# GAT and relational-attention layers: the fourth quad's scores, the masks and the affine steps in other places of a turn

## The chip, the cores and the metric

The kernel runs on one core of one Trainium2 chip. The metric is the device time of one execution in microseconds. The figures below are the times of the kernel before and one execution of it that the hardware profiler took.

## What is computed

The reference runs 64 graphs of 256 nodes with 256 features through two layers in float32. Cut to what matters here:

```python
# layer 0
h = gat(gat(x, adj))                  # two graph attentions, softmax over axis 1
h = layernorm(x + h) * g1 + b1
x = layernorm(h + relu(h @ wf1 + bf1) @ wf2 + bf2) * g2 + b2      # 256 -> 1024 -> 256
# layer 1
q, k = x @ Wq + bq, x @ Wk + bk                                   # 8 heads of 32
attn = softmax(q k^T / sqrt(32))
out = sum over r of (attn * (adj == r)) @ (x @ Wv[r] + bv[r])
x = layernorm(x + out @ Wo + bo) * g1 + beta1
x = layernorm(x + gelu(x @ W1 + b1) @ W2 + b2) * g2 + beta2
```

As `adj` is 0 or 1 here, two relations are enough: the kernel forms `e @ v0 + (e * adj) @ (v1 - v0)` and divides by the sum of `e` afterwards.

## The kernel before

**Turns.** Two graphs make a unit; there are 32 units (NG). `turn(y, x, z)` works on three units at once: the attention and the second layer of unit y, the first feed-forward of unit x = y + 1, the two graph attentions of unit z = y + 2. Turn 0 is the first; turns 1 to 29 have all three units and `middle` true; turn 30 has no z, turn 31 neither z nor x. In the code Y, X and Z are the units' tiles, and `if Z:`, `if X:`, `if middle:` choose between the variants.

**The order.** With `tc.manual_schedule` the instructions of PE (matmul), SP (DMA queue), DVE (vector) and ACT (scalar) go out in the order in which the code traces them; in turn 31 only those of PE and SP. Everything else, POOL (GpSimd) always, and DVE and ACT in turn 31, a planner places by its own costs, and it may slip such an instruction between ordered ones of an earlier turn. `with behind(...)` ties a block to a marked instruction. Buffers of a tag rotate: a new tile takes one that was released and waits for its last reader. The tag "g" has six PSUM banks, "po" and "zo" one each; e, ea and es have two buffers each.

**Attention of unit y.** `Projections` p forms q, k and v with seven products instead of eight; names such as "q5" or "v7" are these steps. Steps 1 and 2 (and 5 and 3; and 1, 6, 7, 4 in the other bank) share a bank: each step accumulates into it after the partial result of the step before has been taken, by an ACT copy (first time for a quarter of the output) or a DVE addition (second time), line 1040 or 1043. The same holds for the steps of the first feed-forward, `hidden_seven`, named "2a", "1a", ... "4b" (number of the product, half of the rows): "h1a" banks hold 1, 6, 7, 4 and "h1b" banks 2, 5, 3; the matmuls are line 900, the additions line 909, the copies line 912. Its moving operands tt are four differences (line 882). "ra" and "rb", "sa" and "sb" apply the activation on ACT.

The attention itself is cut in four **quads** (graph b, half m of the heads), numbers 0 to 3:
- `scores(n)`: 16 matmuls sp on 32x128 tiles (line 1076) into four banks, one for each head, and four exponentials on ACT (line 1085, `powers`), which release the banks;
- `masks(n)`: two DVE products of 128x1024, e with the adjacency (line 1089), for two heads each; `totals(n)`: one DVE addition (line 1094);
- `sums(n)`: 32 matmuls po (line 1104) and 8 matmuls zo (line 1107), on 128x32 tiles;
- `shares(b)`, after the two quads of graph b: `divided`, on DVE a transpose of zo, a reciprocal, a transpose back and a product with po (lines 1115 to 1120), with one addition on POOL (line 1117).

Then `out_(b)` multiplies by Wo. `project(z, ...)` (xpp, line 741) and others belong to unit z. `HiddenOut` out, with steps 1, 2, 5, 6, 3, 7, 4, is the second product of a feed-forward (yf, line 989): `product`, then `add` on DVE (line 997), `sums` for its operands (line 975).

**Norms and affine steps.** `norm` leaves mean and variance, POOL's power (lines 838, 839) the inverse deviation, `offsets` (DVE, line 846) mean times it, `applied_norm` normalizes on ACT (line 856). `affine` is `times` (line 865) and `plus` (line 868), both DVE on 128x1024. `waiting` holds unit y - 1 between its last product and its norm, its affine step and its store (`stored`, one DMA on SP); `late` holds affine steps that a turn leaves to the next: that of unit 0 for turn 0, and those of units 30 and 31 for turn 31. `piece()` is one step of unit 30's last product, done in turn 31.

**Around the change**, a middle turn has this order on PE: q and v steps with sp of quad 0 among them, sp of quad 1, sums 0, 2a 1a 5a, sp of quad 2, sums 1, 6a 3a 2b 1b 7a 5b 6b 4a 3b 7b, sp of quad 3, half of xpp, 4b, sums 2, sums 3, yop.

Of the kernel before, what the change touches and what calls it, by code (L numbers as in the profile page):

```python
# [385 lines left out]
def narrow_path(  # L386
# [22 lines left out]
    T = G * NB  # L409
# [438 lines left out]
    def applied_norm(y, blocks, mv, rs, nm, part=None, gpsimd=False):  # L848
        if part is None:
            offsets(blocks, mv, rs, nm)  # L850
        for t in part or blocks:
            if gpsimd:
                nc.gpsimd.tensor_scalar(y[:, t, :], y[:, t, :], rs[:, t:t + 1], nm[:, t:t + 1],
                                        op0=ALU.mult, op1=ALU.add)
                continue
            mark["normed"] = nc.scalar.activation(y[:, t, :], y[:, t, :], AF.Identity,  # L856
                                                  bias=nm[:, t:t + 1], scale=rs[:, t:t + 1])

    def affine(y, g_, b_):

        times(y, g_)
        plus(y, b_)
# [244 lines left out]
            nc.tensor.matmul(zo[a * DH:(a + 1) * DH, m * N:(m + 1) * N], ones, es[:, a, :],  # L1107
                             start=True, stop=True)

    def divided(u, b, po, zo, oT):  # L1110


        rz = work.tile([P, KB * N], F32, tag="es", name=f"rz{u}_{b}")
        rq = work.tile([P, KB * N // 32], F32, tag="rq", name=f"rq{u}_{b}")
        nc.vector.transpose(rz, zo)
        nc.vector.reciprocal(rq, rz.rearrange("p (n r) -> p n r", r=32)[:, :, 0])  # L1116
        nc.gpsimd.tensor_add(low, low, rq)  # L1117
        nc.vector.transpose(rz.rearrange("p (n r) -> p n r", r=32),
                            rq[:, :, None].to_broadcast([P, KB * N // 32, 32]))
        mark[f"divided{b}"] = nc.vector.tensor_tensor(  # L1120
            oT[:, :, b * N:(b + 1) * N], po.rearrange("p (m n) -> p m n", m=KB),
            rz.rearrange("p (m n) -> p m n", m=KB), ALU.mult)
# [95 lines left out]
    def turn(y_, x_, z):  # L1218
# [4 lines left out]
        q, k_, v = p.qk[:, :, 0], p.qk[:, :, 1], p.v  # L1223
        oT = q
        acc = [None] * G
        e, pe = {}, {}

        def scores(n, heads=range(HPB)):
# [9 lines left out]
        def totals(n):  # L1238
            e[n] = node_sums(*e[n])
# [4 lines left out]
                acc[b] = [psum.tile([P, 512], F32, tag=t_, name=f"{t_}{y_}_{b}") for t_ in ("po", "zo")]  # L1244
            applied(b, m, v, *e.pop(n), *acc[b])

        def shares(b):
            divided(y_, b, *acc[b], oT)

        def out_(b):  # L1250
            add_blocks(y_, "yop", y, b, lambda t, k: oT[:, k, t * P:(t + 1) * P],
# [2 lines left out]
        def first(names, ends=0):  # L1254

            if X:
                steps(names)
            else:
                for _ in range(ends):
                    piece()  # L1260
# [3 lines left out]
                                            ("PE", "SP", "DVE", "Activation")[:4 if X else 2]})  # L1264
        with order:
            p.sums()
            while late:
                affine(*late.pop(0))
            if X:
                n = X.pop("n")  # L1270
                offsets(*n)
# [35 lines left out]
            if X:  # L1307
                masks(0, (0,))
            if middle:
                p("q3 q7 v7")  # L1310
                masks(0, (2,))
            else:
                p("q6 v6 q7 v7")
                if X:
                    masks(0, (2,))
            if X:
                totals(0)
            else:
                with behind("projected"):
                    masks(0)  # L1320
                    totals(0)
            p("v3 q4 v4" if middle else "q4 v4")
            if waiting:
                last = norm(w, 3, wy, mv=last)
# [8 lines left out]
            if waiting:  # L1333
                first("2a 1a")
                applied_norm(wy, *last, [0, 1])
                first("5a")
                applied_norm(wy, *last, [2, 3])
            else:
                first("2a 1a 5a", 1)
            if Z:  # L1340
                early(z)
            scores(2)
            sums(1)
            first("6a")
            if X:
                shares(0)
            first("3a", 1)
            if not X:
                with behind("out"):
                    shares(0)  # L1350
            first("2b ra 1b")
            masks(2, (0,))
            first("7a")
            masks(2, (2,))
            first("5b sa 6b 4a")
            totals(2)
            first("3b rb 7b")
            if X:
                times(X["y"], rg1)
                plus(X["y"], rb1)  # L1360
            scores(3)
            first("sb", 2)
            masks(3)
            totals(3)
            if Z:
                project(z, range(0, T // 2))
            first("4b")
# [33 lines left out]
            if Z:  # L1401
                out(1)
                Z["m"].scores(0)
                Z["m"].scores(1)
                Z["m"].exp(0)
                Z["m"].exp(1)
                out.sums(4)
                offsets(*n)
                out(2)
                applied_norm(y, *n, range(T))  # L1410
                Z["m"].masks(0)
                out(5)
                Z["m"].masks(1)
                Z["m"].shares()
            elif X:
                out.product(5)
                out.sums(3)
                out.add(5)
            if not Z:
                applied_norm(y, *n)  # L1420
            else:
                Z["m"].scaled(WH)
            if Z:
                out.product(6)
                hT = normed_features(y_, 2, y, copied=(1, 2))
                nc.scalar.activation(work.tile([P, 1], F32, tag="ve", name=f"ve{y_}"), mhalf[:, 0:1], AF.Gelu)
                out.add(6)
                out.sums(3)
                out(3)
            elif X:  # L1430
                out(6)
                out.sums(4)
                out(7, 3)
            if not Z:
# [2 lines left out]
                hT = [h.rearrange("p (t a r) -> p t a r", t=T, r=32) for h in hT]  # L1437
                if not X:
                    affine(y, rg3, rb3)
            if waiting:  # L1440
                affine(waiting[0][1], rg4, rb4)
                stored(*waiting.pop(), slice(0, T))
            if z + 1 < NG:
# [16 lines left out]
            if Z:  # L1460
                second("2a 1a")
                n = norm(x_, 1, X["y"], mv=n, rest=range(NB + 1, T))
                second("2b 1b ca 6a")
                offsets(*n)
                applied_norm(X["y"], *n, [0])
                applied_norm(X["y"], *n, [2, 3], True)
                second("5a")
                applied_norm(X["y"], *n, [1])
                affine(y, rg3, rb3)
                second("6b 5b cb")  # L1470
                X["hT"] = normed_features(x_, 1, X["y"], natural=True)
                second("7a 7b sa sb 3a da 3b db 4a 4b")
            else:
                if X:
                    n = norm(x_, 1, X["y"], mv=n, rest=range(NB + 1, T))
                second("2a 1a 2b 1b")
                second("5a 5b")
                if X:
                    offsets(*n)
                    applied_norm(X["y"], *n, [0])  # L1480
                second("3a")
                if X:
                    applied_norm(X["y"], *n, [1])
                second("3b")
                if X:
                    applied_norm(X["y"], *n, [2, 3], True)
                second("6a 6b ca cb da db 7a 7b")
                if X:
                    X["hT"] = with_ones(to_features(X["y"], f"h2T{x_}", (nc.vector.tensor_copy,) * 2))
                second("sa sb 4a 4b")  # L1490
# [131 lines left out]
```

## Time and profile before

| what | value |
|---|---|
| runs | 2994.01, 2994.96, 2993.78 us, median 2994.01 |
| the profiled execution's own time | 2993.49 us |
| its span, first to last instruction | 2991.8 us |
| TensorE's granted clock, mean | 0.995 |
| PE busy | 2950.5 us (99%) |
| DVE, ACT, POOL busy | 2616.8 (87%), 1820.6 (61%), 624.3 (21%) us |
| start of turns 0, 1, 11, 30, 31 (first q product) | 103.78, 199.93, 1107.25, 2831.81, 2905.27 us |

PE is TensorE's matmuls, PEld its weight loads, which overlap them. In a table by stretch each engine has its busy time and, in brackets, its instructions. In a timeline a line has the start, the time from the first start to the last end of the instructions merged in it, the engine, the line of the kernel, the operation, output and inputs, the shapes, the count, and in square brackets the idle time before it and what ended it. Ends of matmuls are modelled, so the text compares starts.

### The profile page before, as it was taken

To read this page: it belongs to the slowest core of one execution; us is meant where nothing else is said; L and a number is where in the kernel's file an instruction comes from. 1 tells how busy PE (TensorE), PEld (TensorE's weight loads), DVE (VectorE), ACT (ScalarE), POOL (GpSimd) and SP (SyncE) were. 2 spreads that over 40 slices of the span, in tenths; PEclk is the share of its full clock that TensorE was granted. 3 is DMA by queue.
4 is the path that set the end of the run, shared out by engine and by line. 5 is a ranking of instruction groups with operands and counts; after the bars stand their busy time and mean duration, and the time that the engine had idled before them with its cause. 6 is when DMAs were issued, how large, how long until landed. Compare 5 with 4: busy or idle time off the path is not lost.

```text
span 2991.8 us, 58459 instructions
## 1 busy us (share of the span) xinstructions
PE 2950.5 (99%) x22192; PEld 2494.1 (83%) x22192; DVE 2616.8 (87%) x5024; ACT 1820.6 (61%) x3803; POOL 624.3 (21%) x930
## 2 busy tenths in 40 slices
PE   7999999999999999999999999999999999999998
PEld 5788888888888888888888888888888888888876
DVE  5789989889898889898889898898988898988887
ACT  4466656656655666666666566566566666666653
POOL 4222111221211221211221112212112212112211
PEclk8999999999999999999999999999999999999999
DMA  5011111111111111111111111111111111111000
GB/s 150 13 29 36 34 36 26 42 34 36 33 31 33 42 34 36 30 27 40 36 37 34 35 26 42 35 37 34 31 33 42 34 36 31 26 40 35 18 11 16
DMA packets 416883, 105.36 MB, mean 35 GB/s; under 512 B 360746, under 2 KB 416084, under 8 KB 416596
## 3 DMA queue, kind: packets, MB, share of 16 engines
q1 hardware_dynamic: 415196, 100.23, 15.3%
q8 instruction: 177, 2.90, 0.4%
q0 software_dynamic: 1056, 1.05, 0.1%
q14 instruction: 110, 0.90, 0.1%
q10 hardware_dynamic: 344, 0.28, 0.0%
HBM read 56.78 MB, written 16.78 MB: 25 GB/s over the span
## 4 chain that ended last, share of the span: by engine, by line
PE 95%; DVE 2%; DMA 1%; ACT 1%; POOL 0%; issue 0%; SPq 0%; DVEq 0%; POOLq 0%; ACTq 0%
PE yf L989 26%; PE h1a L900 15%; PE h1b L900 11%; PE po L1104 8%; PE v L1056 7%; PE qk L1056 6%; PE sp L1076 5%; PE xpp L741 4%; PE yop L812 4%; PE hpp L801 3%; PE ygp L812 3%; PE zo L1107 2%; PE rows L750 1%; DVE st L827 0%; DMA wf<-in_L_gnn_w_ff_dram 0%
## 5 line engine op out<-in xcount | busy, mean ns | idle before, releaser
L1089 DVE TENSOR_TENSOR ea<-e,aT 128x1024 f32<-128x1024 f32 x256 | 307.5, 1213 | 2.8 <-ACT e L1085 2.8
L856 ACT ACTIVATE y<-y,nm,rs 128x256 f32<-128x256 f32 x450 | 242.7, 593 | 95.5 <-DVE nm L846 89.2
L912 ACT COPY h<-h1b 128x512 f32<-128x512 f32 x262 | 153.0, 584 | 223.1 <-PE h1b L900 221.4
L1085 ACT ACTIVATE e<-sp 128x512 f32<-128x512 f32 x512 | 270.8, 598 | 27.4 <-PE sp L1076 20.7
L1043 ACT COPY qk<-qk 128x512 f32<-128x512 f32 x128 | 74.5, 582 | 290.1 <-PE qk L1056 290.1
L918 ACT ACTIVATE h<-h,cols 128x256 f32<-128x256 f32 x512 | 221.7, 501 | 38.5 <-DVE h L909 38.5
L711 POOL COPY hT<-yt 32x256 f32<-32x256 f32 x244 | 211.7, 867 | 139.5 <-DVE yt L694 131.7
L909 DVE TENSOR_TENSOR h<-h1a,h 128x512 f32<-128x512 f32 x262 | 176.1, 681 | 68.3 <-PE h1a L900 64.0
L838 POOL TENSOR_SCALAR rs<-mv 128x4 f32<-128x4 f32 (+1 forms) x134 | 34.2, 255 | 897.8 <-DVE mv L828 480.1
L827 DVE BATCH_NORM_STATS2 st<-y 128x6 f32<-128x256 f32 x512 | 208.0, 408 | 5.6
L997 DVE TENSOR_TENSOR y<-yf,y 128x256 f32<-128x256 f32 x448 | 184.8, 413 | 25.5 <-PE yf L989 25.4
L1117 POOL TENSOR_TENSOR low<-low,rq 128x16 f32<-128x16 f32 x64 | 14.0, 219 | 806.9 <-DVE rq L1116 806.9
L868 DVE TENSOR_TENSOR y<-y,rb 128x1024 f32<-128x1024 f32 (+1 forms) x130 | 167.0, 1285 | 3.2
L743 ACT COPY xp<-xpp 128x260 f32<-128x260 f32 x128 | 45.5, 387 | 194.2 <-PE xpp L741 194.1
L865 DVE TENSOR_TENSOR y<-y,rg 128x1024 f32<-128x1024 f32 (+1 forms) x130 | 155.7, 1198 | 1.2 <-ACT y L856 1.1
L1094 DVE TENSOR_TENSOR es<-e 128x1024 f32<-128x1024 f32 x128 | 155.6, 1216 | 0.0
L839 POOL TENSOR_TENSOR rs<-rs,mhalf 128x4 f32<-128x4 f32 (+1 forms) x134 | 146.2, 1091 | 8.3
L1076 PE MATMUL sp<-qk 32*128 32x256 f32 x2048 | 146.6, 400 | 0.0
L1104 PE MATMUL po<-e,v 128*32 128x256 f32 x2048 | 136.3, 384 | 0.0
L900 PE MATMUL h1a<-tt,wf 128*128 128x256 f32 x512 | 134.5, 386 | 0.3 <-DVE h L909 0.3
L1104 PE MATMUL po<-ea,v 128*32 128x256 f32 x2048 | 134.3, 379 | 0.0
L741 PE MATMUL xpp<-gwe,xT 128*128 128x260 f32 x512 | 128.0, 394 | 2.8 <-ACT xT L675 2.8
(284 smaller groups left out, 7744.3 us busy)
## 6 DMA issues: line engine op xcount, KB each, us to landing
hT<-yt SPq DMA_DIRECT2D x852, 32.0 KB, 1.9
y<-in_x_dram SPq DMA_DIRECT2D x32, 512.0 KB, 4.5
xq<-in_x_dram SPq DMA_DIRECT2D x240, 64.0 KB, 2.2
aq<-in_adj_dram SPq DMA_DIRECT2D x240, 64.0 KB, 2.4
out_dram<-y SPq DMA_DIRECT2D x30, 512.0 KB, 2.8
wf<-in_L_gnn_w_ff_dram SPq DMA_DIRECT2D x2, 1024.0 KB, 7.4
w<-in_L_gnn_W_dram SPq DMA_DIRECT2D x2, 1024.0 KB, 7.6
first<-in_adj_dram POOLq DMA_DIRECT2D x2, 512.0 KB, 7.8
```

Of the source, the lines that this page charges most:

```text
L711: nc.gpsimd.tensor_copy(to, at)
L741: nc.tensor.matmul(ps[:, :WX], hT[k][:, t * P:(t + 1) * P], gwe[:, k, :], start=(k == 0), stop=(k == KB - 1))
L812: nc.tensor.matmul(ps[:, i * F:(i + 1) * F], lhs(t, k), rhs(b, k), start=(k == 0), stop=(k == n - 1))
L856: mark["normed"] = nc.scalar.activation(y[:, t, :], y[:, t, :], AF.Identity, bias=nm[:, t:t + 1], scale=rs[:, t:t + 1])
L900: nc.tensor.matmul(ps[:, i * N:(i + 1) * N], w_[:, f * P:(f + 1) * P], m, start=first and i == 0, stop=True, skip_group_check=True)
L918: nc.scalar.activation(y, y if ps is None else ps[:, i * N:(i + 1) * N], func, bias=bi[:, f:f + 1])
L989: nc.tensor.matmul(s.ps[n][:, i * F2:(i + 1) * F2], a[:, k, i * P:(i + 1) * P], w_[:, k, :], start=n in (1, 2, 5) and i == 0 and k == 0, s ...
L1056: nc.tensor.matmul(ps[:, i * N:(i + 1) * N], l, r, start=n in (1, 2, 5) and i == 0, stop=True, skip_group_check=True)
L1076: nc.tensor.matmul(ps[a][:, j * N:(j + 1) * N], k_[hp, m, j0:j0 + P], q[hp, m, b * N:(b + 1) * N], start=True, stop=True)
L1085: nc.scalar.activation(e[:, a, :], ps[a], AF.Exp, scale=isd)
L1089: nc.vector.tensor_tensor(ea[:, a:a + 2, :], e[:, a:a + 2, :], ab[:, None, :].to_broadcast([P, 2, NB * N]), ALU.mult)
L1104: nc.tensor.matmul(po[hp, m * N:(m + 1) * N], vs[:, hp], w[:, a, j * N:(j + 1) * N], start=(n == 0), stop=(n == len(terms) - 1))
```

## The change

In the order of the code:
- `divided` is split: `reciprocals` (first transpose, reciprocal, POOL's addition) and `divided` (transpose back, product). `shares` takes which of the two.
- `late` affine steps: from the start of the turn to behind the totals of quad 0.
- In a middle turn `times` of unit x goes from behind step 7b to between the two mask products of quad 0; in turn 0 it stays late. `plus` follows the totals of quad 3.
- The second pair of unit y - 1's normalizations goes behind the scores of quad 2.
- The scores of quad 3 go from behind 7b to behind sums 1: sp, then the exponentials of three heads, step 6a, the fourth exponential.
- Masks and totals of quad 2 go ahead of step 3a and so ahead of the division of graph 0; the two parts of that stand behind "ra" and behind 7a. Masks of quad 3 stand before and after steps 3b and 7b.
- Turn 30: step 6 of the first feed-forward's second product goes ahead of a normalization; affine and store of unit 29 go behind steps 5a 5b of the second feed-forward.

```diff
@@ -1107,7 +1107,7 @@
             nc.tensor.matmul(zo[a * DH:(a + 1) * DH, m * N:(m + 1) * N], ones, es[:, a, :],
                              start=True, stop=True)
 
-    def divided(u, b, po, zo, oT):
+    def reciprocals(u, b, zo):
 
 
         rz = work.tile([P, KB * N], F32, tag="es", name=f"rz{u}_{b}")
@@ -1115,6 +1115,10 @@
         nc.vector.transpose(rz, zo)
         nc.vector.reciprocal(rq, rz.rearrange("p (n r) -> p n r", r=32)[:, :, 0])
         nc.gpsimd.tensor_add(low, low, rq)
+        return rz, rq
+
+    def divided(b, po, rz, rq, oT):
+
         nc.vector.transpose(rz.rearrange("p (n r) -> p n r", r=32),
                             rq[:, :, None].to_broadcast([P, KB * N // 32, 32]))
         mark[f"divided{b}"] = nc.vector.tensor_tensor(
@@ -1223,6 +1227,7 @@
         q, k_, v = p.qk[:, :, 0], p.qk[:, :, 1], p.v
         oT = q
         acc = [None] * G
+        shared = {}
         e, pe = {}, {}
 
         def scores(n, heads=range(HPB)):
@@ -1244,8 +1249,12 @@
                 acc[b] = [psum.tile([P, 512], F32, tag=t_, name=f"{t_}{y_}_{b}") for t_ in ("po", "zo")]
             applied(b, m, v, *e.pop(n), *acc[b])
 
-        def shares(b):
-            divided(y_, b, *acc[b], oT)
+        def shares(b, parts=(0, 1)):
+            for n in parts:
+                if n == 0:
+                    shared[b] = reciprocals(y_, b, acc[b][1])
+                else:
+                    divided(b, acc[b][0], *shared[b], oT)
 
         def out_(b):
             add_blocks(y_, "yop", y, b, lambda t, k: oT[:, k, t * P:(t + 1) * P],
@@ -1264,8 +1273,6 @@
                                             ("PE", "SP", "DVE", "Activation")[:4 if X else 2]})
         with order:
             p.sums()
-            while late:
-                affine(*late.pop(0))
             if X:
                 n = X.pop("n")
                 offsets(*n)
@@ -1307,6 +1314,7 @@
             if X:
                 masks(0, (0,))
             if middle:
+                times(X["y"], rg1)
                 p("q3 q7 v7")
                 masks(0, (2,))
             else:
@@ -1319,6 +1327,8 @@
                 with behind("projected"):
                     masks(0)
                     totals(0)
+            while late:
+                affine(*late.pop(0))
             p("v3 q4 v4" if middle else "q4 v4")
             if waiting:
                 last = norm(w, 3, wy, mv=last)
@@ -1334,34 +1344,42 @@
                 first("2a 1a")
                 applied_norm(wy, *last, [0, 1])
                 first("5a")
-                applied_norm(wy, *last, [2, 3])
             else:
                 first("2a 1a 5a", 1)
             if Z:
                 early(z)
             scores(2)
             sums(1)
+            if waiting:
+                applied_norm(wy, *last, [2, 3])
+            scores(3, (0, 1, 2))
             first("6a")
+            powers(3, (3,))
             if X:
-                shares(0)
+                masks(2)
+                totals(2)
             first("3a", 1)
             if not X:
                 with behind("out"):
                     shares(0)
-            first("2b ra 1b")
-            masks(2, (0,))
-            first("7a")
-            masks(2, (2,))
+                masks(2)
+                totals(2)
+            first("2b ra")
+            if X:
+                shares(0, [0])
+            first("1b 7a")
+            if X:
+                shares(0, [1])
             first("5b sa 6b 4a")
-            totals(2)
+            masks(3, (0,))
             first("3b rb 7b")
+            first("sb", 2)
+            masks(3, (2,))
+            totals(3)
             if X:
-                times(X["y"], rg1)
+                if not middle:
+                    times(X["y"], rg1)
                 plus(X["y"], rb1)
-            scores(3)
-            first("sb", 2)
-            masks(3)
-            totals(3)
             if Z:
                 project(z, range(0, T // 2))
             first("4b")
@@ -1416,6 +1434,8 @@
                 out.product(5)
                 out.sums(3)
                 out.add(5)
+            if X and not Z:
+                out(6)
             if not Z:
                 applied_norm(y, *n)
             else:
@@ -1428,7 +1448,6 @@
                 out.sums(3)
                 out(3)
             elif X:
-                out(6)
                 out.sums(4)
                 out(7, 3)
             if not Z:
@@ -1437,7 +1456,7 @@
                 hT = [h.rearrange("p (t a r) -> p t a r", t=T, r=32) for h in hT]
                 if not X:
                     affine(y, rg3, rb3)
-            if waiting:
+            if waiting and Z:
                 affine(waiting[0][1], rg4, rb4)
                 stored(*waiting.pop(), slice(0, T))
             if z + 1 < NG:
@@ -1475,6 +1494,9 @@
                     n = norm(x_, 1, X["y"], mv=n, rest=range(NB + 1, T))
                 second("2a 1a 2b 1b")
                 second("5a 5b")
+                if waiting:
+                    affine(waiting[0][1], rg4, rb4)
+                    stored(*waiting.pop(), slice(0, T))
                 if X:
                     offsets(*n)
                     applied_norm(X["y"], *n, [0])
```

## The prediction

> **What bounds the kernel now.** I read the busy table first, then a table by stretch (one turn in the middle, the first turn, the last but one), then TensorE's timeline of one middle turn, and last that of the other engines beside it.
>
> ```profile
> PE 2950.5 (99%) x22192; PEld 2494.1 (83%) x22192; DVE 2616.8 (87%) x5024; ACT 1820.6 (61%) x3803; POOL 624.3 (21%) x930
> ```
>
> ```profile
> 1016.52:1107.25 90.73, 90.73 (x690) 77.02 (x689) 81.32 (x157) 56.86 (x119) 18.78 (x28) 1.00 0.16 34
> 103.78:199.93 96.15, 93.32 (x690) 77.83 (x691) 82.24 (x149) 54.94 (x115) 24.86 (x32) 0.98 0.14 27
> 2831.81:2905.27 73.46, 70.16 (x538) 56.11 (x537) 60.27 (x108) 37.26 (x72) 12.11 (x20) 1.00 0.05 14
> ```
>
> The columns are length, then PE, PEld, DVE, ACT and POOL busy. A middle turn takes 90.73 us with PE busy in all of it; 27 of the 29 turns between the first and the last two repeat that to 0.01 us, two are some 0.3 us longer. So nothing that the waits list can be won there. But PE's ends are modelled, so I take starts. A 128x128 product of 256 columns starts every 0.216 us, a four-piece step every 0.863 us; whatever start-to-start time lies above that is lost.
>
> ```profile
> 1036.21 1.15 PE L1076 MATMUL sp<-qk 32*128 32x256 f32 x16
> 1037.29 1.07 PE L1104 MATMUL po<-e,v 128*32 128x256 f32 x16
> ...
> 1039.04 0.61 PE L1107 MATMUL zo<-es,ones 128*32 128x256 f32 x8
> 1039.58 1.13 PE L900 MATMUL h1a<-tt,wf1s 128*128 128x256 f32 x4
> ...
> 1044.87 1.03 PE L900 MATMUL h1a<-tt,wf1s 128*128 128x256 f32 x4
> 1045.89 1.13 PE L900 MATMUL h1a<-tt,wf 128*128 128x256 f32 x4
> ...
> 1048.68 1.15 PE L1076 MATMUL sp<-qk 32*128 32x256 f32 x16
> 1049.75 2.02 PE L741 MATMUL xpp<-gwe,xT 128*128 128x260 f32 x8
> ```
>
> Two losses stand here. First, **changes of shape**: sp on quarter tiles has the work of 16 x 0.216 / 4 = 0.86 us and takes 1.08; zo of 8 has 0.43 and takes 0.54. Second, **one wait**: the step from 1044.87 to 1045.89 takes 1.02 instead of 0.86, and the first pieces after it another 0.10. Its cause:
>
> ```profile
> 1044.02 1.22 DVE L1089 TENSOR_TENSOR ea<-e,aT 128x1024 f32<-128x1024 f32 x1
> ...
> 1045.15 0.68 DVE L909 TENSOR_TENSOR h<-h1a,h 128x512 f32<-128x512 f32 x1
> ...
> 1045.89 0.73 PEld L900 LDWEIGHTS h1a<-tt,wf 128*128 128x128 f32 x4 [0.40 <-DVE h L909]
> ```
>
> Step 4a accumulates in the bank that the addition of 7a reads. That addition stands on DVE behind half of masks(2) and ends at 1045.83; 4a could have gone at 1045.73. The loss is 0.16 + 0.10 = 0.26 us a turn.
>
> [...] leaving full shape costs 0.09 and entering sp 0.10; sp to po 0.11 + 0.02; leaving zo 0.11 and entering full shape 0.10. [...] an addition of 128x1024 took 2.02 us beside POOL's weight sums, against 1.30 on average.
>
> **The change in a middle turn.**
> *scores(3) behind sums(1).* Before, sp2 with sums(1) is one visit to quarter tiles (entry 0.19, sp to po 0.13, exit 0.21) and sp3 another (0.19 and 0.21): 0.93 in all. After, they are one visit: 0.19 + 0.13 + seam + 0.21. The seam zo to sp3 is not in the trace. It lies between 0 (zo to the next po in sums(2), sums(3) loses nothing) and 0.11 + 0.10 = 0.21 (zo's exit, sp's entry). I take 0.21: saved 0.93 - 0.74 = 0.19, at most 0.40.
> *Does sp3 find its banks?* Six banks: two are held by steps 2a/5a and 1a, four by sp2, so sp3 waits for all four exponentials of quad 2. Where ACT is free they start 1.17 us after sp (1029.97 to 1031.14) and go as follows:
>
> ```profile
> 1031.14 2.06 ACT L1085 ACTIVATE e<-sp 128x512 f32<-128x512 f32 x4 [0.47 <-PE sp L1076]
> ```
>
> Before, those of quad 2 began only at 1037.80, behind two normalizations of 1.09. The change puts these behind the exponentials: start 1036.21 + 1.17 = 1037.38, end 1039.44. sp3 can start at 1039.47 to 1039.58. It just fits; I take a wait of 0, and keep 0 to 0.25 (half of one exponential's spacing of 0.49). A gain below 0 is excluded, since a wait cannot be negative.
> *ACT after that.* Normalizations 1039.34 to 1040.45, three exponentials from sp3's 1039.58 + 1.17 = 1040.75 to 1042.3, copy of 6a to 1042.8, fourth exponential to 1043.3, copy of 2b to 1044.14. PE wants them at 1044.2 (7a) and 1045.08 (5b): slack 1.4 and 0.94.
> *Masks(2) and totals(2) ahead of 3a's addition and of the division.* DVE had waited 0.48 for zo and 0.62 for 1b. In the new order, at spacings of 1.13 for 128x1024 and 0.61 for 128x512: the transpose of xq to 1039.26, masks and totals to 1042.65, addition of 3a at 1042.76, first half of the division (0.75 + 0.29) to 1044.41, 1b's addition to 1045.17, 7a's to 1046.03, second half (0.75 + 0.61) to 1047.32. PE, shifted, wants 1b's at 1045.95 (6b) and 7a's at 1046.81 (4a). Both are met by 0.78, so the 0.26 goes. masks(3) ends at 1051.4, sums(3) wants it at 1055.1. The division's one POOL addition (0.22 us) has POOL idle for 17 us behind it.
> *The affine product beside the value products.* 1.25 us of DVE after masks(0,(0,)), where DVE idles 1.40 us for the qk products: nothing, and if that cover were gone, 1.25 on q3's addition. It also leaves the late place: DVE reaches the next zo some 0.7 us before PE delivers it.
> *Sum:* 0.19 + 0.26 = **0.45 us a turn**, bounds 0.20 (bank wait 0.25) and 0.66 (free seam). 29 turns: **-13.1** (-5.8 to -19).
>
> **The end turns.**
> *Turn 0.* PE loses 2.99 + 0.10 us here:
>
> ```profile
> 108.15 2.02 DVE L868 TENSOR_TENSOR y<-y,rb 128x1024 f32<-128x1024 f32 x1
> ...
> 111.96 1.13 PE L1056 MATMUL qk<-tq,wqks 128*128 128x256 f32 x4 [2.83 <-DVE qk L1040]
> ```
>
> The affine step (106.90 to 110.17) stands ahead of q2's addition, for which q5 waits. Moved behind totals(0), the offsets come at 107.25 to 109.1 (POOL's weight sums may hold them) and the addition at 109.0 to 109.9; q5 goes at 109.1 to 110.0: saved 2.0 to 2.9, I take 2.4. In the new place its 2.4 us push DVE back behind a transfer that it awaited anyway (0.83 idle); about 0.25 comes back as waits for 1b's addition. With 0.45 from above: **-2.6**.
> *Turn 30.* 0.45 as above; masks(3) earlier ends the stall in sums(3) (0.60 and 0.10); out(6) ahead of the normalization puts addition 6 (2882.62) before the offsets that waited for POOL, and product 7 comes at 2882.56 instead of 2883.09: 0.53; the affine step of turn 29 leaves the place before the four differences tt, where DVE does 4.87 us of such steps and PE stalls 1.58 + 0.08: 1.66; the stall of 0.93 behind it shrinks by 0.6. Against it: with sp3 gone and no project in this turn, 4b follows 7b at once and waits for its addition: 0.2 + 0.69 + 0.06 and 0.1 restart, -1.1 of gain. The store (one transfer of 512 KB on SP) moves with the affine step; SP has nothing due behind it but later stores, so nothing. Sum **-2.8**, bounds -1 to -4: the planner may still slip turn 31's affine steps in there.
> *Turn 31.* q5 waits 1.43 + 0.10 behind affine and other early work: about 1.4 back; one shape change 0.19. DVE and ACT are planned here, not ordered, so bounds +1.5 to -3: **-1.6**.
>
> **The sum** against the profiled execution (2993.49 us; span 2991.8 and 1.7 around it): 13.1 + 2.6 + 2.8 + 1.6 = 20.1. The median of the runs, 2994.01, is 0.5 longer: 2994.0 - 20.1 = **2974**.
>
> **Rivals.**
> *The new seam eats its gain (B).* sp3 waits 0.25 for banks, weight loads included. For it: the margin is 0.03 to 0.14 us. Against: where ACT was free the start was the same 1.17 each time. Middle turns give 0.20: 2994 - 5.8 - 7 = 2981.
> *End turns give nothing (C)*, because the planner puts other steps in the places left: 2994 - 13 = 2981.
> *ACT becomes the wait (D, slower).* Place: the copy of 2b, queued behind sp3's exponentials, and 5b that needs it. It decides when ACT is over 0.94 us late; each turn then loses what is above. At 2 us late, the price is 1.06 + 0.1 restart: 2994 + 29 x (1.16 - 0.45) - 7 = 3008. For it: 6a's and 2b's copies now stand behind up to four exponentials. Against: ACT is busy 56.86 of 90.73 and idled 0.91 and 1.14 us at those copies.
> *The change does not do what it says (E)*: the reordered instructions leave PE's starts as they are, for instance because 4a waits for something else next; DVE is at 81.32 of 90.73 and could keep it so: 2990.
>
> **How the numbers follow.** Forecast 0.68, B 0.11, C 0.08, D 0.06, E 0.07. Low: 0.6 x 29 in the middle and 9.5 at the ends is 27, so 2967; high: 0.2 x 29 and 3 is 9, so 2985. That takes in B and C. A measurement can tell about 0.2% (6 us). Faster: forecast, B, C, 0.87; the same: E, 0.07; slower: D, 0.06.
>
> **What would show it.** Middle turns of 90.3 us; one visit sp, po, zo, sp with no full step between; the first exponential of quad 2 about 1.17 us after its sp; no PEld wait for DVE h at 4a; q5 of turn 0 without the 2.83; in turn 30 a new wait of about 1 us at 4b. Wrong, if middle turns stay at 90.7 or above, or if PE waits for an ACT copy in the first-layer steps.

## The result, and the profile after

The changed kernel takes 2977.29 us (median of 5 runs, 2977.13 to 2978.8) against 2994.01: ratio 0.9945, 95% interval 0.993 to 0.9959. Forecast was 2974, with 2967 to 2985 as the range. The profiled execution has a span of 2975.6 us, 16.3 less than before.

The page's first line, then the table by stretch: a middle turn, turn 0, turn 30, and turn 31 to the end.

```profile
PE 2936.1 (99%) x22192; PEld 2501.2 (84%) x22192; DVE 2624.7 (88%) x5024; ACT 1822.6 (61%) x3803; POOL 635.6 (21%) x930
```

```profile
1008.87:1099.13 90.26, 90.26 (x690) 77.23 (x689) 81.68 (x157) 56.94 (x119) 19.24 (x28) 1.00 0.16 35
103.58:196.46 92.88, 92.88 (x690) 78.01 (x690) 80.43 (x149) 54.87 (x115) 23.13 (x32) 0.98 0.14 28
2814.50:2886.94 72.44, 69.18 (x539) 56.20 (x538) 60.56 (x108) 37.26 (x72) 13.00 (x20) 1.00 0.05 14
2886.94:2975.60 88.66, 70.81 (x587) 57.32 (x585) 61.54 (x115) 34.84 (x70) 7.83 (x19) 0.95 0.04 14
```

No engine has instructions added or removed (the counts are those of before); only the order differs, so lengths are compared. Counted from the first q product of a turn to that of the next:

| stretch | before | after | measured | forecast |
|---|---|---|---|---|
| up to turn 0 | 103.78 | 103.58 | -0.20 | 0 |
| turn 0 | 96.15 | 92.88 | -3.27 | -2.6 |
| turns 1 to 29 | 2631.88 | 2618.03 | -13.85 | -13.1 |
| turn 30 | 73.46 | 72.44 | -1.02 | -2.8 |
| turn 31 to the end | 86.57 | 88.62 | +2.05 | -1.6 |
| sum | | | -16.3 | -20.1 |

**The middle** is as forecast. TensorE's timeline of the same turn as in the prediction, in the kernel after:

```profile
1028.56 1.15 PE L1076 MATMUL sp<-qk 32*128 32x256 f32 x16
1029.64 1.07 PE L1104 MATMUL po<-e,v 128*32 128x256 f32 x16
...
1031.39 0.61 PE L1107 MATMUL zo<-es,ones 128*32 128x256 f32 x8
1031.93 1.15 PE L1076 MATMUL sp<-qk 32*128 32x256 f32 x16
1033.01 1.13 PE L900 MATMUL h1a<-tt,wf1s 128*128 128x256 f32 x4
...
1038.29 1.03 PE L900 MATMUL h1a<-tt,wf1s 128*128 128x256 f32 x4
1039.16 1.03 PE L900 MATMUL h1a<-tt,wf 128*128 128x256 f32 x4
```

Sp, po, zo and sp are one visit to quarter tiles. Eight zo take 0.54 instead of 0.43 and sp again 1.08, so the seam costs 0.11 + 0.10 = 0.21, the value that the forecast took. Step 4a (1039.16) follows 6b (1038.29) after 0.87 us, with no wait. ScalarE's timeline there:

```profile
1029.79 2.06 ACT L1085 ACTIVATE e<-sp 128x512 f32<-128x512 f32 x4 [0.53 <-PE sp L1076]
1031.71 1.10 ACT L856 ACTIVATE y<-y,nm,rs 128x256 f32<-128x256 f32 x2
1033.15 1.58 ACT L1085 ACTIVATE e<-sp 128x512 f32<-128x512 f32 x3 [0.33 <-ACT y L856]
...
1035.90 0.59 ACT L912 COPY h<-h1b 128x512 f32<-128x512 f32 x1 [0.20 <-PE h1b L900]
```

The exponentials of quad 2 begin 1.23 us after sp (forecast 1.17) and end at 1031.85; sp of quad 3, at 1031.93, loses nothing to them. The copy of 2b ends 27.6 us into the turn, where the forecast had it too.

**Turn 0** lost its stall. TensorE, then VectorE:

```profile
108.96 1.13 PE L1056 MATMUL qk<-tq,wqks 128*128 128x256 f32 x4
```

```profile
107.06 0.16 DVE L846 SCALAR_TENSOR_TENSOR nm<-mv,rs 128x4 f32<-128x4 f32 x1 [0.26 <-POOL rs L839]
108.21 0.69 DVE L1040 TENSOR_TENSOR qk<-qk,qk 128x512 f32<-128x512 f32 x1 [0.99 <-PE qk L1056]
```

The addition for q5 now waits for TensorE's q2, not the other way round. The other executions repeat it: counted from the turn's start, q5 begins at 8.2 us in all six kernels with the affine step at its old place, and at 4.3 or 5.4 us in all eight with it moved.

**Turn 30** has two waits to explain. TensorE's timeline, then VectorE's and ScalarE's around the second:

```profile
2848.31 1.13 PE L900 MATMUL h1a<-tt,wf 128*128 128x256 f32 x4 [0.78 <-DVE h L909]
...
2878.53 1.89 PE L900 MATMUL h1a<-tt,w1s 128*128 128x256 f32 x8
2882.39 2.10 PE L900 MATMUL h1a<-tt,w 128*128 128x256 f32 x8 [1.96 <-DVE h L909]
```

```profile
2877.96 1.22 DVE L865 TENSOR_TENSOR y<-y,rg 128x1024 f32<-128x1024 f32 x1
2879.21 1.23 DVE L868 TENSOR_TENSOR y<-y,rb 128x1024 f32<-128x1024 f32 x1
2880.35 0.15 DVE L846 SCALAR_TENSOR_TENSOR nm<-mv,rs 128x4 f32<-128x4 f32 x1
2881.64 0.69 DVE L909 TENSOR_TENSOR h<-h1a,h 128x512 f32<-128x512 f32 x1 [1.14 <-ACT h L912]
```

```profile
2880.54 0.60 ACT L856 ACTIVATE y<-y,nm,rs 128x256 f32<-128x256 f32 x1 [3.03 <-DVE nm L846]
2881.05 0.56 ACT L912 COPY h<-h1b 128x512 f32<-128x512 f32 x1
```

The first is the new wait at 4b, as forecast. The second is read backwards: step 7a of the second feed-forward waits for the addition of 6a, the addition for a copy on ACT, the copy stands behind a normalization on ACT, the normalization waits for the offsets nm, and these stand on DVE behind the affine step that the change put there (2877.96 to 2880.44). The same two steps in the kernel before:

```profile
2898.07 1.89 PE L900 MATMUL h1a<-tt,w1s 128*128 128x256 f32 x8
2900.73 2.11 PE L900 MATMUL h1a<-tt,w 128*128 128x256 f32 x8 [0.76 <-DVE h L909]
```

Eight such pieces take 1.73 where nothing waits, so this place lost 0.93 before and 2.13 after.

**Turn 31** keeps the old wait of q5 and has a new one ahead of sums 2. TensorE, then VectorE:

```profile
2891.82 1.13 PE L1056 MATMUL qk<-tq,wqks 128*128 128x256 f32 x4 [1.27 <-DVE qk L1040]
...
2916.66 1.95 PE L989 MATMUL yf<-w2t,wq 128*128 128x128 f32 x16
2920.68 1.07 PE L1104 MATMUL po<-e,v 128*32 128x256 f32 x16 [2.08 <-DVE qk L1124]
```

```profile
2914.24 2.36 DVE L1089 TENSOR_TENSOR ea<-e,aT 128x1024 f32<-128x1024 f32 x2 [1.01 <-ACT e L1085]
...
2916.85 0.71 DVE L1115 STREAM_TRANSPOSE rz<-zo 128x512 f32<-128x512 f32 x1
...
2919.95 0.68 DVE L1124 TENSOR_TENSOR qk<-po,rz 128x512 f32<-128x512 f32 x1
```

Sums 2 needs the po bank that the product of graph 0 (line 1124) reads. The planner has put the masks of quad 3 ahead of that division, since their scores are now early and were late before. Start to start 2.24 us are lost here; the kernel before lost 0.09 at the same place, the price of the change of shape:

```profile
2935.19 1.95 PE L989 MATMUL yf<-w2t,wq 128*128 128x128 f32 x16
2937.07 1.07 PE L1104 MATMUL po<-e,v 128*32 128x256 f32 x16
```

### The profile page after: what moved, and what is told of

Its sections match the earlier page's. It is cut to its first block, busy times and chain, and to the rows that moved or that the text cites. A ratio compares the mean times of both kernels' runs of the same rounds, so it can differ in the third digit from the quotient of the medians.

```text
span 2975.6 us, 58457 instructions
## 1 busy us (share of the span) xinstructions
PE 2936.1 (99%) x22192; PEld 2501.2 (84%) x22192; DVE 2624.7 (88%) x5024; ACT 1822.6 (61%) x3803; POOL 635.6 (21%) x930
## 3 DMA queue, kind: packets, MB, share of 16 engines
q0 software_dynamic: 1056, 1.05, 0.1%
## 4 chain that ended last, share of the span: by engine, by line
PE 96%; DVE 2%; ACT 1%; DMA 1%; issue 0%; POOL 0%; SPq 0%; POOLq 0%; DVEq 0%; ACTq 0%
PE yf L989 26%; PE h1a L900 15%; PE h1b L900 11%; PE po L1104 8%; PE v L1056 7%; PE qk L1056 6%; PE sp L1076 5%; PE yop L812 4%; PE xpp L741 4%; PE hpp L801 4%; PE ygp L812 3%; PE zo L1107 2%; PE rows L750 1%; DMA wf<-in_L_gnn_w_ff_dram 0%; DVE s L776 0%
## 5 line engine op out<-in xcount | busy, mean ns | idle before, releaser
L1085 ACT ACTIVATE e<-sp 128x512 f32<-128x512 f32 x512 | 277.2, 606 | 51.7 <-PE sp L1076 35.8
L711 POOL COPY hT<-yt 32x256 f32<-32x256 f32 x244 | 237.4, 973 | 139.0 <-DVE yt L694 131.4
L865 DVE TENSOR_TENSOR y<-y,rg 128x1024 f32<-128x1024 f32 (+1 forms) x130 | 162.0, 1246 | 1.2 <-ACT y L856 1.1
L839 POOL TENSOR_TENSOR rs<-rs,mhalf 128x4 f32<-128x4 f32 (+1 forms) x134 | 134.6, 1004 | 8.4
L1076 PEld LDWEIGHTS sp<-qk 32*128 32x128 f32 x2048 | 92.5, 184 | 47.6 <-ACT e L1085 12.8
```

Source lines behind the costliest of these rows:

```text
L711: nc.gpsimd.tensor_copy(to, at)
L1076: nc.tensor.matmul(ps[a][:, j * N:(j + 1) * N], k_[hp, m, j0:j0 + P], q[hp, m, b * N:(b + 1) * N], start=True, stop=True)
L1085: nc.scalar.activation(e[:, a, :], ps[a], AF.Exp, scale=isd)
```

## The experiments

Two questions: why the middle came out as forecast (so that it is not luck), and what the ends lost. All lengths are us from first q product to first q product.

| run | turn 0 | middle turn | turn 30 | turn 31 to end | span | time, runs |
|---|---|---|---|---|---|---|
| scores alone | 98.55 | 91.47 | 74.54 | 88.85 | 3018.4 | 3021.53, 4 |
| scores and masks 3 | 96.74 | 91.30 | 74.65 | 90.28 | 3014.2 | 3016.77, 4 |
| scores and times | 96.92 | 90.53 | 73.69 | 88.60 | 2989.5 | 2991.94, 12 |
| DVE order alone | 97.50 | 90.47 | 73.20 | 86.87 | 2985.8 | 2988.30, 12 |
| norms first | 92.29 | 90.56 | 72.74 | 90.85 | 2987.1 | 2988.53, 13 |
| times late | 92.29 | 90.28 | 72.45 | 88.65 | 2974.7 | 2976.09, 4 |
| late steps first | 97.31 | 90.27 | 74.03 | 88.27 | 2980.7 | 2982.30, 1 |
| division first | 92.28 | 90.27 | 72.45 | 86.95 | 2972.8 | 2974.41, 1 |
| turn 30 mended | 92.88 | 90.27 | 69.45 | 88.52 | 2973.0 | 2974.65, 1 |
| three end edits | 92.27 | 90.27 | 69.31 | 87.83 | 2970.4 | 2973.12, 5 |
| both ends | 92.26 | 90.27 | 69.45 | 86.97 | 2969.4 | 2972.98, 5 |
| late steps third | 92.87 | 90.27 | 69.31 | 86.93 | 2971.8 | 2971.99, 4 |

The lengths are of the one execution that was profiled; the last column has the median of all runs of that kernel and their number. Some lengths outside the middle hold 3.41 us at half clock by the clock records of their traces (granted 0.50; last section): turn 31 of "scores and masks 3" and of "norms first", turn 0 of "scores alone" and "DVE order alone", turns 0 and 30 of "late steps first", and the start of turn 0 in six kernels, the kernel before and the changed one among them.

**Scores alone.** The kernel before, with only the scores of quad 3 (and the normalizations) moved.

```diff
                 first("5a")
-                applied_norm(wy, *last, [2, 3])
...
             sums(1)
+            if waiting:
+                applied_norm(wy, *last, [2, 3])
+            scores(3, (0, 1, 2))
             first("6a")
+            powers(3, (3,))
...
-            scores(3)
             first("sb", 2)
```

> The kernel before with the scores of quad 3 alone moved behind sums 1, and the second pair of normalizations behind the scores of quad 2; DVE's order is that of before. Theory: one visit to quarter tiles less is worth 0.19 us a middle turn, the wait of 0.26 at 4a stays: 90.54 us a turn. With 4b now next to 7b in turn 30 (+0.9) and the planner's order in turn 31 (+2) the total is about 2991 us. Rival: the new place of the scores is worth the whole gain, DVE's order nothing: 90.27 us a turn.

Measured: 91.47 a middle turn, time ratio 1.009 (1.0073 to 1.0107): slower, and neither theory had it. The seam gave its 0.20 and the wait at 4a stayed, but sums 3 lost 0.16 and yop 0.79 (the expectations of the next two runs have 0.24 for sums 3; start to start it is 0.16). VectorE's timeline, and TensorE's yop of graph 1:

```profile
1051.23 0.69 DVE L909 TENSOR_TENSOR h<-h1b,h 128x512 f32<-128x512 f32 x1 [0.68 <-ACT h L912]
1052.84 0.69 DVE L909 TENSOR_TENSOR h<-h1a,h 128x512 f32<-128x512 f32 x1 [0.92 <-PE h1a L900]
...
1067.01 0.71 DVE L1115 STREAM_TRANSPOSE rz<-zo 128x512 f32<-128x512 f32 x1
```

```profile
1069.62 1.97 PE L812 MATMUL yop<-wo,qk 128*128 128x256 f32 x8 [0.56 <-DVE qk L1120]
```

Counted from the turn's start, 1b's addition (the line at 1052.84) is at 27.98, where it was at 26.89: sp of quad 3 now stands ahead of 1b on TensorE, and DVE, whose order is that of the code, waits 1.09 longer. From there to the division of graph 1 it has next to no idle time, so that division starts 1.08 later too (42.15 for 41.07), and yop finds it late. DVE had become the bound of that stretch. The next two kernels test this.

**Scores and masks 3.** As above, with the masks of quad 3 earlier.

```diff
             totals(2)
+            masks(3, (0,))
             first("3b rb 7b")
+            first("sb", 2)
+            masks(3, (2,))
+            totals(3)
             if X:
                 times(X["y"], rg1)
                 plus(X["y"], rb1)
-            first("sb", 2)
-            masks(3)
-            totals(3)
```

> The scores of quad 3 behind sums 1 in the kernel before, with the masks of quad 3 before and after steps 3b and 7b and its totals ahead of times and plus; masks of quad 2 and the division of graph 0 stay where they were. With the scores moved alone a middle turn took 91.47 us. Theory: what was lost there is DVE's idle time. Sp of quad 3 now stands ahead of step 1b, so DVE waits about 1.1 us longer for the copy of 2b and for the product of 1b, has no idle time after that until the division of graph 1, and comes that much late to yop; the order of its work between does not matter. Then the loss in sums 3 goes (0.24), but the wait at yop grows by as much: 91.4 to 91.5 a middle turn, time about 3021. Rival: the masks of quad 3 stood too late, and that is all: 90.5 a middle turn, time about 2993.

Measured: 91.30. The loss in sums 3 is gone, but 0.26 lie at 4b, whose additions now stand behind a mask product, and 0.50 at yop: this order of the same work moves the wait, and takes 0.17 off it. The rival, 90.5, falls. The theory's cause holds, its number (91.4 to 91.5) was missed by 0.1, since yop's wait shrank where it had said that it would grow.

**Scores and times.** The scores, and `times` where DVE idled 1.40 us.

```diff
             if middle:
+                times(X["y"], rg1)
                 p("q3 q7 v7")
...
             if X:
-                times(X["y"], rg1)
+                if not middle:
+                    times(X["y"], rg1)
                 plus(X["y"], rb1)
```

> The scores of quad 3 behind sums 1 in the kernel before, and times of a middle turn between the two mask products of quad 0, where DVE idles 1.40 us; the rest stays. Theory: DVE's late stretch from 1b's addition to the division of graph 1 gets 1.25 us shorter, which is more than the 1.03 that PE waited there (0.24 in sums 3, 0.79 at yop): both waits go, the wait at 4a stays, and a middle turn takes 90.73 - 0.19 = 90.54, up to 90.6; time about 2993 with turn 0 still long. Rival: the order of masks 3 and of the division decides: above 91 a middle turn, time above 3008.

Measured: 90.53, the theory's number; the total can't be told from that of the kernel before (ratio 0.9984 to 1.0001), as the ends take back more than half of the gain: turn 31 alone is 2.0 longer. DVE still waits 0.92 for 1b, but has 1.25 us less to do behind it, and TensorE loses nothing at sums 3 and yop. The scores are worth 0.20 of 90.73 once DVE can follow.

**DVE order alone.** Masks and totals of quad 2 ahead of 3a, and the division in two parts, in the kernel before.

```diff
-                shares(0)
+                masks(2)
+                totals(2)
...
-            first("2b ra 1b")
-            masks(2, (0,))
-            first("7a")
-            masks(2, (2,))
+            first("2b ra")
+            if X:
+                shares(0, [0])
+            first("1b 7a")
+            if X:
+                shares(0, [1])
             first("5b sa 6b 4a")
-            totals(2)
...
```

> The kernel before with DVE's new order alone: masks and totals of quad 2 ahead of step 3a and of the division, the division in two parts; the scores of quad 3 at their old place. Theory: without the 1.08 us of sp of quad 3 ahead of 6a, PE reaches 1b and 6b that much earlier while DVE has 3.4 us of masks in front, so the wait leaves 4a and comes back at 6b: 90.65 to 90.75 us a turn, total about 2993 us. Rival: the two parts add up (0.26 here, 0.19 for the scores): 90.47 us a turn, total about 2986 us.

Measured: 90.47, the rival's number and not the theory's: 0.26 a turn, the whole wait at 4a and nothing back at 6b; ratio 0.9977 (0.9968 to 0.9986). The step ahead of 4a, then 4a, on TensorE:

```profile
1043.45 1.03 PE L900 MATMUL h1a<-tt,wf1s 128*128 128x256 f32 x4
1044.32 1.03 PE L900 MATMUL h1a<-tt,wf 128*128 128x256 f32 x4
```

Scores 0.20 and order 0.26 add up to the 0.46 of the changed kernel.

**Norms first.** The changed kernel, the second pair of normalizations back ahead of the exponentials of quad 2.

```diff
                 first("5a")
+                applied_norm(wy, *last, [2, 3])
...
             sums(1)
-            if waiting:
-                applied_norm(wy, *last, [2, 3])
             scores(3, (0, 1, 2))
```

> The changed kernel with the second pair of normalizations back ahead of the scores of quad 2. Theory: the exponentials of quad 2 then begin 0.42 us later and end 0.26 us after sp of quad 3 could start, which needs all four banks: 90.5 to 90.6 us a middle turn, total about 2986 us. Rival: the banks have slack and the new place of the normalizations is worth nothing: 90.27 us, 2977 us.

Measured: 90.56, +0.29, and all of it inside sp of quad 3. TensorE's timeline:

```profile
1033.37 1.43 PE L1076 MATMUL sp<-qk 32*128 32x256 f32 x16
1034.73 1.13 PE L900 MATMUL h1a<-tt,wf1s 128*128 128x256 f32 x4
```

It takes 1.36 to the next start instead of 1.08. In the trace the exponentials of quad 2 end 0.34 later than in the changed kernel, and of the 16 pieces only the four of the last head start later, by 0.29: they wait for the last bank. Sp as a whole begins as soon after zo as in the changed kernel, so its start there was the seam's and not a bank's. So the banks are a real limit, and the place of the normalizations is what keeps it away.

**Times late.** The changed kernel with `times` back behind 7b (its two lines moved back).

> The changed kernel with the affine product of middle turns back behind the totals of quad 3. Theory: both places are covered, as DVE is ahead of PE by about 0.7 us at the end of the attention and the 1.25 us more make it late by 0.5 us only for a division that PE wants 3.6 us later: 90.27 us a middle turn, total 2977 us within 1. Rival: DVE becomes the wait at the second half of the attention: up to 0.5 us a turn, 2992 us.

Measured: 90.28, no difference beyond 0.01. With the changed order of masks and division DVE's idle time ahead of 3a is 0.27 and none lies ahead of 1b, so the place of `times` is free here, while with the scores alone it was worth 0.94.

**Late steps first.** The changed kernel, in turn 0 the affine step of unit 0 at the start again.

```diff
             p.sums()
+            while late and X:
+                affine(*late.pop(0))
```

> The changed kernel with the affine step of unit 0 back at the start of turn 0 (turn 31 as changed). Theory: q5 of turn 0 waits for q2's addition behind it again, turn 0 takes 95.7 us instead of 92.9 and everything behind it is as after: about 2980 us. Rival: turn 0 gained for another reason (its first matmuls): below 94 us.

Measured: turn 0 97.31, 4.43 above the changed kernel. q5 started 8.21 us into the turn, as in the kernel before (8.18), so the cause is confirmed: 2.83 of the 4.43. The rest of the excess lies right behind that idle time of 4.07 us, at half clock: the 16 sp took 2.02 instead of 1.08 to the next start, the four pieces after them 1.58 instead of 0.96. Turn 30, with nothing changed in it, was 1.59 longer in this execution, also at half clock in part (granted 0.63 from 2886 to 2890 us; last section).

**Division first.** The changed kernel, the masks of quad 3 in turn 31 tied behind the division of graph 0 (the totals, which don't need the masks, are not tied).

```diff
-            masks(3, (0,))
+            if X:
+                masks(3, (0,))
             first("3b rb 7b")
             first("sb", 2)
-            masks(3, (2,))
+            if X:
+                masks(3, (2,))
+            else:
+                with behind("divided0"):
+                    masks(3)
             totals(3)
```

> The changed kernel with the masks of quad 3 tied behind the division of graph 0 in turn 31 alone, where the planner had slipped them ahead of it. Theory: the wait of 2.24 us in front of sums 2 of turn 31 was DVE's order, it falls below 0.9 us, the total by 1.4 to 2.2 us, to about 2975.5 us. Rival: the division is held by its tie to the addition of unit 30's last product, which itself comes later now: the wait stays above 1.8 us.

Measured: turn 31 is 86.95, 1.67 less; the wait ahead of sums 2 fell from 2.24 to 0.62. On VectorE the masks now follow the product of the division:

```profile
2917.22 0.69 DVE L1124 TENSOR_TENSOR qk<-po,rz 128x512 f32<-128x512 f32 x1
...
2918.16 2.35 DVE L1089 TENSOR_TENSOR ea<-e,aT 128x1024 f32<-128x1024 f32 x2
```

The planner's order was the cause of 1.62 of it; the rest stays.

**Turn 30 mended.** The changed kernel, with 4b behind sums 3 and the affine step behind the normalization and the copies after it.

```diff
-            first("4b")
+            if Z:
+                first("4b")
             sums(2)
             sums(3)
+            if not Z:
+                first("4b")
...
                 second("5a 5b")
-                if waiting:
-                    affine(waiting[0][1], rg4, rb4)
-                    stored(*waiting.pop(), slice(0, T))
...
                     X["hT"] = with_ones(to_features(X["y"], f"h2T{x_}", (nc.vector.tensor_copy,) * 2))
+                if waiting:
+                    affine(waiting[0][1], rg4, rb4)
+                    stored(*waiting.pop(), slice(0, T))
```

> The changed kernel with two edits in turn 30 alone: the affine step and store of unit 29 behind the copies of the transposed x instead of ahead of the offsets, and step 4b behind sums 3. Theory: the wait of 2.13 us ahead of 7a falls below 0.4 us and that of 0.95 us at 4b goes: turn 30 takes 69.2 to 69.8 us instead of 72.44; turn 31 may lose up to 1 us at q5: total about 2974.5 us. Rival: 7a waits for something else at nearly the same time (POOL's power, the copy on ACT): turn 30 above 71 us.

Measured: turn 30 is 69.45, 2.99 less, and turn 31 no longer than in the changed kernel. Both waits shown above were local: that at 4b is gone, and of the 2.13 ahead of 7a 0.18 is left.

**Three end edits.** The last two together, and in turn 31 the late affine steps tied behind q2's addition, so that q5 need not wait for them.

```diff
                 p("v2")
+                mark["started"] = mark["projected"]
...
+                with behind("started"):
+                    while late:
+                        affine(*late.pop(0))
```

> The changed kernel with the edits of turns 30 and 31 together, and the affine steps of turn 31 tied behind its first two additions of the projections, so that the planner can't put them ahead of q2's. Theory: 1.4 to 2.2 us from the division, 3 us from turn 30, 0.5 to 1.4 us at q5, which the affine steps may cost again at q3: about 2972 us. Rival: the planner puts other work in those places and the total stays above 2975 us.

Measured: q5's wait fell from 1.43 to 0.30, but the affine steps now delayed later additions of the q and v steps (1.61 and 0.34 us of wait on TensorE): turn 31 is 87.83, above the 86.95 without the tie.

**Both ends.** The same without that tie.

> The changed kernel with two ends mended together, without a tie for the late affine steps: in turn 31 the masks and totals of quad 3 only behind the division of graph 0; in turn 30 the affine step and store of unit 29 behind the normalization of the second feed-forward's input instead of ahead of its offsets, and 4b behind sums 3. Theory: both losses are local and add up: turn 30 takes 69.4 us as it did with the second edit alone, turn 31 86.9 as with the first alone, the middle 90.27; span about 2969.5 to 2970, time about 2971.5, ratio to the kernel before 0.992. Rival: the steps that the planner slips in at turn 30 move with the affine step, and turn 31 loses again what turn 30 gains: turn 31 at 88 or more, time 2973 or more, as in the run with all three edits.

Measured: 69.45 and 86.97, span 2969.4, each edit at its own size; the median of the runs, 2972.98 (2970.39 to 2973.81), is above the 2971.5 that was expected. Ratio to the kernel before 0.9928 (0.9914 to 0.9941).

**Late steps third.** Both ends, and the late steps of turn 31 traced behind the totals of quad 1, tied behind the last addition of the q and v steps.

```diff
             totals(1)
+            with behind("projected"):
+                while late:
+                    affine(*late.pop(0))
             sums(0)
...
```

> As the kernel with both ends mended, and in turn 31 the two late affine steps tied behind the last addition of the q and v steps and traced behind the totals of quad 1. Theory: q5's wait of 1.43 us in turn 31 comes from the planner's early affine step and squares; without them it falls to about 0.3, and the four affine instructions (4.9 us) find DVE idle for only 1.6 and 1.9 us near the first sums, so 0.5 to 1.5 us come back as waits for masks: turn 31 between 86.3 and 87.5. Turn 30 loses two slipped affine instructions and is at 69.4 or up to 1 us less. Time 2970 to 2972. Rival: the tied steps go ahead of the masks of quads 0 and 1 and cost PE 2 us or more there: turn 31 at 88.5 or above, time 2973 or more.

Measured: q5's wait 0.30, and in its place 1.48 instead of 0.62 ahead of sums 2. TensorE's timeline:

```profile
2888.65 1.13 PE L1056 MATMUL qk<-tq,wqks 128*128 128x256 f32 x4
...
2916.76 1.07 PE L1104 MATMUL po<-e,v 128*32 128x256 f32 x16 [1.31 <-DVE qk L1124]
```

Turn 31 is 86.93, 0.04 less than without. From 2898.82 up to the division of graph 0 DVE now has no idle time, so what was taken from q5 comes back at sums 2. The times of the last three kernels (ratios 0.9927, 0.9928, 0.9924) cannot be told apart.

## Why the prediction was right, and where it was not

**The total** lies in the range because the middle carries it: the middle gave 13.85 for 13.1, the four other stretches 2.4 where 7.0 was forecast.

**The middle, right by its own steps.** The seam was taken at 0.21 and costs 0.21; the bank wait was taken at 0 and is 0, and "norms first", where those exponentials end 0.34 later, shows how close it was (0.29); the 0.26 at 4a went and nothing came in its place. Per turn 0.466 against 0.45. 29 x 0.466 is 13.5; the other 0.35 is that one turn and not two was longer by 0.3. What the forecast did not see is how narrow DVE's part was. It gave the moved `times` no worth, which holds for the changed kernel ("times late"), but not where the order of masks stays; and none of its rivals named DVE late at yop: "scores alone" shows that the same move of scores costs 0.74 a turn when DVE's order is left. The order of masks and division did two things, and the forecast counted one: it ends the wait at 4a, and it fills the idle time that the moved scores would open ahead of 1b. One reading is loose, without harm to a sum: a matmul of the code stands as two pieces in the trace, so 0.216 us is the spacing of pieces, a product takes two of them, and the counts of matmuls in the text are of pieces.

**Rivals B and D** fell: no bank wait, and the copies on ACT were in time. **E** fell, since TensorE's starts did move. **C** came half true: turn 30 and turn 31 together cost 1.0, but turn 0 gave its gain.

**Turn 0**: forecast -2.6. The stall's term was mis-sized: q5 lost 2.99 before and 0.16 after, 2.83 and not 2.4, because POOL held the offsets only 0.26 us; and the 0.25 taken back at 1b did not show.

**Turn 30**: of the forecast's six terms five hold: the middle's gain 0.45; sums 3 0.63 (forecast 0.70); step 6 of the output 0.52 (forecast 0.53); the affine step of unit 29 out of the way of the differences tt 1.66; 4b's new wait -1.05 (forecast -1.1). The failed step is "the stall of 0.93 behind it shrinks by 0.6". It grew by 1.20, since the affine step went to a place just ahead of the offsets on which ACT, and through ACT's order the copies of that feed-forward, depend. The terms sum to 0.45 + 0.63 + 0.52 + 1.66 - 1.20 - 1.05 = 1.01, measured 1.02. "Turn 30 mended" takes the two losses away but for 0.18 and gains 2.99.

**Turn 31**: the 0.19 of one change of shape came. The failed step is "about 1.4 back" at q5: the wait there is still 1.43, since the planner put the late affine step ahead of q2's addition at the old place in the code and at the new one alike. Two ties that held it back did not win the time either: in "late steps third" 1.13 of the wait goes and 0.86 comes back at sums 2. The other loss, 2.24 ahead of sums 2, was no step of the forecast; only its upper bound of +1.5 for a planned turn pointed there, and the turn came to +2.05. "Division first" shows the cause: 1.67 back.

## What to carry to other kernels

When a block of work on the bounding engine is moved forward, look at which product it now stands ahead of: an engine that waits for that product gets idle time (here 1.09 us more on DVE), and what it has queued from there to its next meeting with the bounding engine decides whether the move gains or loses (here +0.74 or -0.20 us a turn for the same move). A step put into a new place must be followed through the next engine's queue as well, to whoever waits behind the instruction that it delays. Where a planner places instructions, an earlier input can change its choice; tie the order that matters.

## What the runs showed of the hardware

- **TensorE's clock behind three waits.** In turn 30 of "late steps first" TensorE idled 1.98 us ahead of 7a (by modelled ends, as all such times here) and ran at half clock from 2887.03 to 2890.45 (granted 0.63 in the mean from 2886 to 2890 us, 0.89 from 2890 to 2892); in the changed kernel it idled 1.96 us at the same place and was granted 1.00 from 2882 to 2890 us. In the kernel before it idled 2.83 us in turn 0 and was granted 1.00 from 107.15 to 200 us. What decides between them was not shown. In the profiled executions of the kernel before and the changed one, the half-clock stretches in the first 108 us are 6.83, 3.41, 10.24 and 3.41 us long (granted 0.50), the same in both.
- Before turn 0 the same code took 102.63 to 104.69 us in different executions. Turn 0 itself took 92.87 or 92.88 in the three executions with the new order whose turn 0 begins at half clock, the changed kernel's among them, and 92.26 to 92.29 in the five others. Differences of 1 us between single executions are therefore not read as effects; the lengths of middle turns, most of which repeat to 0.01 us, are.
- Inside one visit to quarter tiles, in a middle turn of the changed kernel, sp to po costs 0.13 and zo to sp 0.21; zo to po of the same shape costs nothing (sums 2 to sums 3: the eight zo take 0.43 to the next start).
